# An expert FFN in float32: the first products of 64-row blocks as two halves of 32 rows in four column groups

## The chip, the cores and the metric

The kernel runs on one NeuronCore of a Trainium2 chip. Its engines are TensorE (PE in the profile; its weight loads are PEld), VectorE (DVE), ScalarE (ACT), GpSimd (POOL) and SyncE (SP), which issues most of the transfers. The metric is the device time of one execution in microseconds. Three runs of the kernel before took 1034.02, 1034.72 and 1036.19 us; the median is 1034.72 us.

## What is computed

The program takes 625 nodes of 768 features and 20,000 edges, and computes two residual layers in float32. The first is a graph attention network of two layers. The second is a transformer block: causal attention with 12 heads, then a mixture of 8 experts of which each row uses one. The change lies in the experts:

```python
gate_logits = h2 @ Wg
w, sel = jax.lax.top_k(gate_logits, 1)
hid = jax.nn.relu(jnp.einsum('nd,edf->enf', h2, W1) + b1[:, None, :])   # 768 -> 3072
y = jnp.einsum('enf,efd->end', hid, W2) + b2[:, None, :]                # 3072 -> 768
moe = jnp.einsum('ne,end->nd', combine, y)
```

The kernel computes for each row only the expert that it chose. The weights of an expert, W1 and W2, are 9.4 MB each.

## The kernel before

The early part of the program, up to the choice of the experts at about 630 us, is not touched. By then the rows have been written to memory sorted by expert. The first expert's first 128 rows are computed in straight code (`first_step`). All other rows go through a loop (L1498) whose number of passes and whose branches depend on the data: each pass handles one expert, with a block of 128 rows, one of 64, or none, and before it, as the table says, a block of 32. One word of the table says which (`w & 2`: 64 rows, `w & 4`: 128, `w & 1`: 32).

SBUF holds one set of an expert's weights, as six pieces: `w1[0..2]` and `w2[0..2]`, each for 1024 of the 3072 hidden features. As soon as PE no longer needs a half of a piece, SP issues the transfer of the next expert's half into the same place (`load_first` for W1, L1110, in halves of three of the six k; `load_second` for W2, L1120). These transfers are conditional: where the next pass uses the same expert they move nothing.

A 64-row block goes through class `Wide` with M = 64, P = 2 column groups. `into` (L1187) makes the first products: the stationary operand is 64 rows of `xT`, the moving one 512 columns of W1, and two such products lie side by side in the two column groups, with the result in PSUM as rows by hidden features (128 partitions are 2 x 64 rows). VectorE copies this to SBUF (`hb`, L1190). `turn` (L1198) transposes it on TensorE, four 128x128 tiles for each 1024 hidden features, since the second product needs the hidden features on the partitions; ScalarE then adds the bias and applies ReLU on the way from PSUM to `hT` (L1203). `out_of` (L1213) makes the second products with 64 columns of `hT` as the stationary operand, accumulating all three pieces in `pw`. The order on PE is written out by hand: `begin` is into(0), into(1), turn(0), into(2); then comes the block of 32, if there is one; `end` is out_of(0), turn(1), turn(2), out_of(1), out_of(2).

The block of 32 rows (`narrow`) already works in another way: with 32 rows as the stationary operand, four products of 256 columns lie in four column groups (L1461), and one VectorE instruction (L1463) turns the whole result in blocks of 32x32 out of PSUM, so that there is no copy and no turn on TensorE. ScalarE then adds the bias and applies ReLU in place (L1465). Its second products are at L1476.

The order of instructions is by hand for PE and SP; the other engines' order is made by the scheduler. Branches are taken by each engine's own sequencer: L1511 is the one before the 64-row `begin`, L1518 the one before the 32-row block, L1541 the one before the 64-row `end`.

Of the kernel before, what the change touches and what calls it, by code (L numbers as in the profile page):

```python
# [9 lines left out]
F32 = mybir.dt.float32  # L10
# [4 lines left out]
AF = mybir.ActivationFunctionType  # L15
# [10 lines left out]
KD = D // 128  # L26
# [15 lines left out]
B = 128  # L42
NS = E + N // B
SHUFFLE = (0, 3, 2, 4, 1, 5, 6, 7)
Q = 32
# [5 lines left out]
NFC = DF // FC  # L51
NK = DF // 128
BH = E * NK // 2
BLK = FC // 128
# [11 lines left out]
def gnn_moe_kernel(ctx: ExitStack, tc: tile.TileContext, p, out):  # L66
    nc = tc.nc
# [26 lines left out]
    def halves(name, w, k, n):  # L94

        r = k // 2 * 128
        return [wload(f"{name}{i}", k // 2, n,
                      w[i * r:(i + 1) * r, :].rearrange("(k p) n -> p k n", p=128))
                for i in range(2)]
# [51 lines left out]
    with tc.tile_pool(name="gnn", bufs=1) as gp:  # L151
# [31 lines left out]
        with tc.tile_pool(name="oneh", bufs=12) as op_, \  # L183
# [15 lines left out]
            w1 = halves("w1", p["L0_gnn_W1"], KD, HC)  # L199
# [253 lines left out]
            with tc.If(ok == 0):  # L453

                nc.vector.memset(C, 0.0)
                for a in range(0, EJ, PART):
                    clear()
                    for q in range(a, a + PART):
                        g, j = q // GJ, q % GJ
                        ohs = step(past[:, g, j:j + 1], True)  # L460
                        ohd = target(N, dst[:, g, j:j + 1], upper[:, g, j:j + 1])
                        for t in range(T):
                            nc.tensor.matmul(cps[:, t, :SH + 1], ohd[:, cols(t)], ohs, start=False,
                                             stop=False, skip_group_check=True)
# [14 lines left out]
        with tc.tile_pool(name="gw", bufs=2, reuse_waits="tile") as gw, \  # L479
# [13 lines left out]
            class Messages:  # L493


                def __init__(self, t, heads):
                    self.t, self.heads = t, heads
                    self.neg = gw.tile([R, N], F32, name="neg", bufs=1)
                    nc.vector.tensor_scalar(self.neg, C[:, t, :], 0.0, NEG, op0=OP.is_equal,
                                            op1=OP.mult)  # L500
                    self.tot = small.tile([R, HEADS], F32, name="tot")
                    self.z, self.zT, self.agg = {}, {}, None
# [45 lines left out]
            w2 = halves("w2", p["L0_gnn_W2"], KH, D)  # L548
# [93 lines left out]
            tp = ps.tile([128, 8, 128], F32, tag="p2", name="tpa")  # L642
# [54 lines left out]
    with tc.tile_pool(name="att", bufs=1, reuse_waits="tile") as a1, \  # L697
# [11 lines left out]
        def head_weights(name, w, which=(0, 1)):  # L709
            got = []  # L710
            for i in which:
                t_ = wp.tile([128, 3072], F32, tag="w", name=f"{name}{i}")
                v_ = t_[:, :KD * 384].rearrange("p (k n) -> p k n", k=KD)
                for k in range(KD):
                    nc.sync.dma_start(
                        v_[:, k, :].rearrange("p (h s) -> p h s", h=6),
                        w[6 * i:6 * i + 6, k * 128:(k + 1) * 128, :].rearrange("h p s -> p h s"))
                got.append(v_)
            return got
# [11 lines left out]
        hT = ap.tile([128, KD, N], F32, tag="xT", name="hT")  # L731
# [37 lines left out]
        v = a1.tile([R, T, D], F32, name="v")  # L769
        w = head_weights("L0_ffn_Wv", p["L0_ffn_Wv"])  # L770
        for t in range(T):
            for i in range(2):
                pp = ps.tile([128, 512], F32, tag="p1", name="pv")
                for c in range(KD):
                    nc.tensor.matmul(pp[:R, :384], hT[:, c, cols(t)], w[i][:, c, :],
                                     start=(c == 0), stop=(c == KD - 1))
# [326 lines left out]
    w1, w2 = [None] * NFC, [None] * NFC  # L1103
# [27 lines left out]
    sp = ctx.enter_context(tc.tile_pool(name="sps", bufs=2, space=PSUM, reuse_waits="tile"))  # L1131
# [10 lines left out]
    hT = [mw.tile([128, 4, 128], F32, name=f"hT{c}", bufs=1) for c in range(2 * NFC)]  # L1142
    pw = [sp.tile([128, 512], F32, name=f"pw{i}", bufs=1) for i in range(2)]
# [21 lines left out]
    class Wide:  # L1165
# [53 lines left out]
        def begin(self):  # L1219
            self.into(0)  # L1220
            self.into(1)
            for c in range(2, self.n):
                self.turn(c - 2)
                mm = self.into(c)
            return mm

        def end(self):
            n = self.n
            self.out_of(0)
            self.turn(n - 2)  # L1230
            self.turn(n - 1)
            for c in range(1, n):
                mm = self.out_of(c)
            return mm

    def prepare(rows, idx, M):

        nc.vector.tensor_copy(idx[:M], rows.bitcast(I32)[:M, D:D + 1])
        nc.vector.tensor_add(rows[:M, :D], rows[:M, :D], b2b[:M])
# [50 lines left out]
    bT, _ = biases(first_a)  # L1290
# [15 lines left out]
    for i, n in ((0, T), (1, TA)):  # L1306
        for s in range(n):
            nc.tensor.matmul(pc[:1, i * E:(i + 1) * E], ones[:, :1], oh[:, s, :], start=(s == 0),
                             stop=(s == n - 1))

    def row8(name, *shape, tag=None):
        return ap.tile([1, *shape], F32, name=name, tag=tag or name)
# [7 lines left out]
    v = nc.vector  # L1320
# [10 lines left out]
    key = row8("key", E)  # L1331
# [31 lines left out]
    for i in range(3):  # L1363
        s = 1 << i
        a = row8(f"inc{i}", E)
# [29 lines left out]
    begin, n_first, odd, its_number, from_row = (its[:, i, :] for i in range(5))  # L1395
# [16 lines left out]
    a = tabf[:, 0, :]  # L1412
    v.scalar_tensor_tensor(a[:, :NS], its_number, 2.0, tabf[:, 1, :NS], op0=OP.mult, op1=OP.add)
    w = tabf[:, 2, :NS]
# [11 lines left out]
    xT = free[:, U * Q * KD:2 * U * Q * KD].rearrange("p (k r) -> p k r", k=KD)  # L1426
# [26 lines left out]
    def narrow(bT, *then):  # L1453

        def into(c):
            ph = sp.tile([128, 4, 128], F32, tag="tp", name="phq").rearrange("p a b -> p (a b)")[:, :BLK * Q]
            w = w1[c].rearrange("p k (j g r) -> p k j g r", g=4, r=Q)
            v = ph.rearrange("p (j r) -> p j r", r=Q)
            for k in range(KD):
                for g in range(4):  # L1460
                    nc.tensor.matmul(v[g * Q:(g + 1) * Q], xT[:, k, :Q], w[:, k, :, g],  # L1461
                                     start=(k == 0), stop=(k == KD - 1))
            turned = nc.vector.transpose(hq[:, c * BLK:(c + 1) * BLK], v)  # L1463
            for j in range(c * BLK, (c + 1) * BLK):
                nc.scalar.activation(hq[:, j, :], hq[:, j, :], AF.Relu, bias=bT[:, j:j + 1])  # L1465
            return turned

        with tc.manual_schedule(engines={PE}):
            for c in range(NFC):
                turned = into(c)  # L1470
        load_first(*then)
        with tc.manual_schedule(engines={PE}):
            order = [(c, j, i) for c in range(NFC) for j in range(0, BLK, 4) for i in range(2)]
            for c, j, i in sorted(order, key=lambda o: o[0] and 1 + o[2]):
                for g in range(4):
                    nc.tensor.matmul(  # L1476
                        pq[i][g * Q:(g + 1) * Q, :384], hq[:, c * BLK + j + g, :],
                        w2[c][:, j + g, i * 384:(i + 1) * 384], start=(c == 0 and j == 0),
                        stop=(c == NFC - 1 and j == BLK - 4))
        with tc.issue_after(turned.ins):  # L1480
            prepare(rq, iq, Q)
        yq = rq[:, :D].rearrange("p (i c) -> p i c", i=2)
        for i in range(2):
            nc.vector.tensor_add(rs[:, i, :], yq[:, i, :], pq[i][:2 * Q, :384])  # L1484
            nc.vector.tensor_add(rs[:, i, :], rs[:, i, :], pq[i][2 * Q:, :384])  # L1485
            nc.vector.tensor_add(yq[:Q, i, :], rs[:Q, i, :], rs[Q:, i, :])  # L1486
# [11 lines left out]
    with tc.For_i(0, n_blk, 1, iteration_sync="reg_based") as i:  # L1498
        w = word(i)
        then = (w >> 4) & 7, (w >> 3) & 1  # L1500
        row, row_next = (nc.values_load(table[0:1, 1, ds(k, 1)], engines=[pool], min_val=0,
                                        max_val=NR - U * Q) for k in (i, i + 1))

        rows_in(row_next)
        nc.gpsimd.dma_start(rw, xr[ds(row + Q, B), :])
        nc.gpsimd.dma_start(rq[:Q], xr[ds(row, Q), :])
        bT, s = biases((w >> 8) & 7)
        tc.add_manual_dep(s.ins, first_load.ins.name, ORDER)
        of = {M: Wide(M, xT[:, :, Q:Q + M], bT) for M in (64, B)}

        with tc.If((w & 2) == 2) as c64:  # L1511
            with tc.manual_schedule(engines={PE}):
                of[64].begin()
        with c64.Else():
            with tc.If((w & 4) == 4):
                with tc.manual_schedule(engines={PE}):
                    of[B].begin()
        with tc.If((w & 1) == 1) as c32:  # L1518
            narrow(bT, *then)
        with c32.Else():  # L1520
            nc.vector.memset(iq, N)
            load_first(*then)
        turn_next()

        def scatter_narrow(*others):
            s = scatter_out(rq, iq, Q)
            for o in others:
                tc.declare_no_dep(s.ins, o.ins, reason="other rows")
            tc.add_manual_dep(s.ins, first_load.ins.name, ORDER)

        def finish(M):
            prepare(rw, iw, M)
            with tc.manual_schedule(engines={PE}):
                of[M].end()
            load_second(*then)
            add_up(rw, pw, M)
            s = scatter_out(rw, iw, M)
            tc.add_manual_dep(s.ins, first_made.ins.name, ORDER)
            scatter_narrow(s)

        with tc.If((w & 2) == 2) as d64:  # L1541
            finish(64)
        with d64.Else():
            with tc.If((w & 4) == 4) as d128:
                finish(B)
            with d128.Else():
                nc.gpsimd.dma_start(idle, xr[0:1, :8])
                load_second(*then)
                scatter_narrow()
# [31 lines left out]
```

## Time and profile before

The profiled execution took 1035.84 us; its span, from the first to the last instruction, is 1034.0 us, with a mean granted TensorE clock of 0.983.

| | busy us | share of the span | instructions |
|---|---|---|---|
| PE (matmul) | 971.3 | 94% | 4655 |
| PEld (weight loads) | 595.9 | 58% | 4656 |
| DVE | 460.1 | 44% | 1340 |
| ACT | 301.5 | 29% | 753 |
| POOL | 76.9 | 7% | 129 |

The DMA queues moved 195.07 MB in all, 174.78 of it on queue q1, which carries the weights. In the profile a line such as `688.12 10.52 PE L1187 MATMUL ph<-ew,xid 128*64 128x512 f32 x48 [0.99 <-SPq L1498]` is read as follows: start in us from the start of the span, duration of the merged group, engine, line of the kernel, operation, what is written and read, the shape of the stationary operand (128 deep by 64 columns) and of the moving one (128x512), how many instructions, and in brackets how long the engine was idle before and what ended that. In the groups of instructions the numbers after the bar are busy time in us, mean ns of one, and idle time before. In the windows the last three columns are granted TensorE clock, busy share of the 16 DMA engines, and GB/s. A float32 product appears as two matmul records and two weight loads.

### The profile page before, as it was taken

What the parts mean: (1) busy time and instruction counts of PE and PEld (TensorE: products, weight loads), DVE (VectorE), ACT (ScalarE), POOL (GpSimd) and SP (SyncE); (2) the same over time, 40 slices, a digit from 0 to 9 for tenths busy, and PEclk for the clock granted to TensorE, in tenths of its full rate; (3) what the DMA queues carried; (4) which work ended last, traced back from release to release, by engine and by line L of the source; (5) the groups of instructions that cost most, each with busy time, mean ns of one, the idle gap of its engine ahead of it and who ended that gap; (6) DMA issues with size and microseconds to landing.
All of it is one profiled execution on the core that took longest, in us unless ns stands there. A gap on an engine that the chain in (4) does not pass through costs nothing. (4 is left out here: it accounts for less than half of the span.)

```text
span 1034.0 us, 14964 instructions
## 1 busy us (share of the span) xinstructions
PE 971.3 (94%) x4655; PEld 595.9 (58%) x4656; DVE 460.1 (44%) x1340; ACT 301.5 (29%) x753; POOL 76.9 (7%) x129
## 2 busy tenths in 40 slices
PE   6888999999999999999999889999999999999992
PEld 4455466577555555677775655545454646644552
DVE  7877697275376660284555464112111213111212
ACT  6667554263140120344442211101110121102020
POOL 1200100000000010000000021010101010110010
PEclk9999999999999999999999889999999999999997
DMA  9300410300150081999400579410689999999991
GB/s 280 148 1 1 165 31 1 138 1 1 48 104 1 20 210 36 364 413 381 181 1 1 203 241 352 151 42 15 236 314 321 388 375 409 367 374 402 409 388 33
DMA packets 86880, 195.07 MB, mean 189 GB/s; under 512 B 32989, under 2 KB 34660, under 8 KB 86825
## 3 DMA queue, kind: packets, MB, share of 16 engines
q1 hardware_dynamic: 80073, 174.78, 47.2%
q0 software_dynamic: 6672, 19.44, 6.1%
q8 instruction: 29, 0.48, 0.2%
q14 instruction: 26, 0.21, 0.1%
q10 hardware_dynamic: 80, 0.16, 0.1%
HBM read 213.34 MB, written 39.55 MB: 245 GB/s over the span
## 5 line engine op out<-in xcount | busy, mean ns | idle before, releaser
L1213 PE MATMUL pw<-ew,hT 128*64 128x384 f32 (+1 forms) x672 | 160.2, 488 | 4.9 <-PEq L1518 2.0
L1213 PEld LDWEIGHTS pw<-ew,hT 128*64 128x64 f32 (+1 forms) x672 | 100.0, 160 | 59.5 <-issue 15.8
L1187 PE MATMUL ph<-ew,xid 128*64 128x512 f32 (+1 forms) x432 | 127.7, 594 | 1.8 <-SPq L1498 1.0
L1203 ACT ACTIVATE hT<-tph,bT 128x64 f32<-128x64 f32 (+1 forms) x168 | 41.0, 361 | 288.5 <-PE tph L1198 194.4
L1187 PEld LDWEIGHTS ph<-ew,xid 128*64 128x64 f32 (+1 forms) x432 | 53.6, 155 | 65.1 <-issue 58.1
L1190 DVE COPY hb<-ph 128x512 f32<-128x512 f32 x30 | 20.6, 691 | 137.0 <-PE ph L1187 137.0
L533 PE MATMUL agg<-xl,zT 125*125 125x256 f32 (+1 forms) x300 | 79.8, 417 | 1.3 <-ACT zT L522 1.1
L533 PEld LDWEIGHTS agg<-xl,zT 125*125 125x125 f32 x300 | 54.5, 188 | 19.6 <-ACT zT L522 2.6
L1250 DVE TENSOR_TENSOR rw<-rw,pw 64x192 f32<-64x192 f32 (+1 forms) x48 | 12.9, 315 | 106.0 <-PE pw L1213 105.7
L360 PE MATMUL pp<-w,yT 128*125 128x512 f32 x120 | 56.0, 606 | 0.0
L235 ACT ACTIVATE step<-iota,past 125x314 f16<-125x314 f16 x120 | 55.9, 548 | 0.0
L633 PE MATMUL ph<-wr,h1T 128*125 128x384 f32 x160 | 52.8, 486 | 0.0
L595 PE MATMUL ph<-w,h1T 128*125 128x384 f32 x160 | 52.4, 486 | 0.0
L252 PE MATMUL cps<-step,oh 125*125 125x314 f16 x181 | 37.1, 307 | 10.5 <-ACT step L235 7.4
L857 DVE CUSTOM_DVE_ANT_0 e<-sc,later 125x625 f32<-125x625 f32 (+4 forms) x60 | 29.8, 542 | 36.2 <-PE sc L841 36.2
L924 PE MATMUL po<-wpj,aT 128*125 128x384 f32 x120 | 42.8, 505 | 0.4 <-DVE xx L928 0.4
L861 ACT ACTIVATE e<-e,of 125x625 f32<-125x625 f32 (+4 forms) x60 | 35.7, 596 | 23.3 <-DVE of L857 23.2
L170 PE MATMUL ph<-wr,yT 128*125 128x512 f32 x96 | 42.1, 593 | 0.1
L595 PEld LDWEIGHTS ph<-w,h1T 128*125 128x125 f32 x160 | 30.0, 188 | 21.2 <-issue 0.5
L245 DVE TENSOR_SCALAR oh<-iota,drel,upper 125x125 f16<-125x125 f16 x160 | 41.1, 316 | 2.2 <-PE cps L252 2.1
L633 PEld LDWEIGHTS ph<-wr,h1T 128*125 128x125 f32 x160 | 29.8, 188 | 20.8
L252 PEld LDWEIGHTS <-oh 125*125 125x125 f16 x181 | 24.9, 140 | 26.6 <-DVE oh L245 13.6
(344 smaller groups left out, 1336.4 us busy)
## 6 DMA issues: line engine op xcount, KB each, us to landing
ew<-in_L_ffn_W_dram SPq DMA_DIRECT2D x108, 1536.0 KB
xr<-zt SPq DMA_DIRECT2D x5, 3076.0 KB
xg<-zt SPq DMA_DIRECT2D x5, 3072.0 KB
w<-in_L_gnn_W_dram SPq DMA_DIRECT2D x4, 1536.0 KB
wr<-in_L_gnn_Wr_dram SPq DMA_DIRECT2D x4, 1536.0 KB
xid<-xg POOLq DMA_DIRECT2D x32, 120.0 KB, 6.5
b2b<-in_L_ffn_b_dram SPq DMA_DIRECT2D x9, 384.0 KB
rw<-xr POOLq DMA_DIRECT2D x7, 384.5 KB, 7.8
```

What stands on the lines that cost most here:

```text
L170: nc.tensor.matmul(pp[:R, :], yT[:, c, cols(t)], part(wr1, KD, c, i, 512), start=(c == 0), stop=(c == KD - 1))
L235: nc.scalar.activation(o, iota[:, :SH + 1], AF.Sign, bias=at, scale=-1.0)
L245: m = nc.vector.tensor_scalar(o, iota[:, :n], at, weight, op0=OP.is_equal, op1=OP.mult)
L252: nc.tensor.matmul(where, target(R, d[:, j:j + 1], w[:, j:j + 1]), step(s[:, j:j + 1], j % 4 != 3), start=False, stop=False, skip_group_ch ...
L360: nc.tensor.matmul(pp[:R, :], yT[:, c, cols(t)], part(w1, KD, c, i, 512), start=(c == 0), stop=(c == KD - 1))
L533: nc.tensor.matmul(self.agg[:R, c0:c0 + n], zT[:, s, :], xl[:, s, x0:x0 + n], start=(s == 0), stop=(s == T - 1))
L595: nc.tensor.matmul(ph[:R, :384], h1T[:, c, cols(t)], part(w2, KH, c, i, 384), start=(c == 0), stop=(c == KH - 1))
L633: nc.tensor.matmul(ph[:R, :384], h1T[:, k, cols(t)], part(wr2, KH, k, i, 384), start=(k == 0), stop=(k == KH - 1))
L924: nc.tensor.matmul(po[t, i][:R, :384], aT[:, c, cols(t)], wpj[i][:, c, :], start=(c == 0), stop=(c == KD - 1))
L1187: mm = nc.tensor.matmul(ph[g * M:(g + 1) * M, :C].rearrange("p (j f) -> p j f", f=128), self.xT[:, k, :], w[:, k, g], start=(k == 0), stop ...
L1203: self.made = nc.scalar.activation(hT[c][:, k, r], tp[:, k, r], AF.Relu, bias=self.bT[:, f:f + 1])
L1213: mm = nc.tensor.matmul(pw[i][g * M:(g + 1) * M, :384], hT[c][:, k, g * M:(g + 1) * M], w[:, self.block(c, g, k), i * 384:(i + 1) * 384], ...
```

## The change

Class `Halves` takes the place of `Wide` for blocks of 64 rows. For each piece of 1024 hidden features it makes the first products twice, once for rows 0 to 31 and once for rows 32 to 63, in four column groups (`into32`, which is also what the block of 32 now calls). VectorE turns each half's result out of PSUM into `hT`, 64 columns for each 128 hidden features; ScalarE adds the bias and applies ReLU in place in SBUF. `begin` now makes all three pieces, and `end` only the second products; their shapes, 64 columns by 384, stay, with other pairs of 128 features side by side. The copies to `hb` and the turns on TensorE are gone for these blocks. Blocks of 128 rows and the straight code are as before.

```diff
+    def into32(c, ph, cols, xT):
+        w = w1[c].rearrange("p k (j g r) -> p k j g r", g=4, r=Q)
+        v = ph[:, :BLK * Q].rearrange("p (j r) -> p j r", r=Q)
+        for k in range(KD):
+            for g in range(4):
+                nc.tensor.matmul(v[g * Q:(g + 1) * Q], xT[:, k, cols], w[:, k, :, g],
+                                 start=(k == 0), stop=(k == KD - 1))
+        return v
+
+    class Halves:
+
+        def __init__(self, xT, bT):
+            self.xT, self.bT = xT, bT
+
+        def begin(self):
+            for c in range(NFC):
+                h = hT[c].rearrange("p a b -> p (a b)").rearrange("p (j r) -> p j r", j=BLK)
+                for r in (slice(0, Q), slice(Q, 2 * Q)):
+                    nc.vector.transpose(h[:, :, r], into32(c, sp.tile([128, 512], F32, name="ph"), r,
+                                                           self.xT))
+                for j in range(BLK):
+                    f = c * BLK + j
+                    nc.scalar.activation(h[:, j, :], h[:, j, :], AF.Relu, bias=self.bT[:, f:f + 1])
+
+        def end(self):
+            M = 2 * Q
+            for c in range(NFC):
+                h = hT[c].rearrange("p a b -> p (a b)").rearrange("p (j r) -> p j r", j=BLK)
+                order = [(j, i) for j in (0, 4, 1, 5) for i in range(2)]
+                for j, i in sorted(order, key=lambda o: o[1]) if c == NFC - 1 else order:
+                    for g in range(2):
+                        nc.tensor.matmul(
+                            pw[i][g * M:(g + 1) * M, :384], h[:, j + 2 * g, :],
+                            w2[c][:, j + 2 * g, i * 384:(i + 1) * 384], start=(c == 0 and j == 0),
+                            stop=(c == NFC - 1 and j == 5))
...
-        of = {M: Wide(M, xT[:, :, Q:Q + M], bT) for M in (64, B)}
+        of = {64: Halves(xT[:, :, Q:Q + 64], bT), B: Wide(B, xT[:, :, Q:Q + B], bT)}
```

More of the change, by code (lines that the diff above doesn't have):

```diff
@@ L1455, in into @@
         def into(c):
[L1456 to L1462, printed above, removed]
+            ph = sp.tile([128, 4, 128], F32, tag="tp", name="phq").rearrange("p a b -> p (a b)")
+            v = into32(c, ph, slice(0, Q), xT)
             turned = nc.vector.transpose(hq[:, c * BLK:(c + 1) * BLK], v)
```

## The prediction, made before the changed kernel ran

> **What bounds the kernel now.** I read the page's slices first (PE at 9 to the end, DMA at 9 from about 775 us), then the order of PE's work in the expert loop, then the busy time by stretch, then the branches. The loop makes seven passes: 64 rows (from 688 us), 128 (723), 64 (789), 64+32 (823), 64 (876), 128+32 (911), 32 (997). So four passes use the changed code. PE in order of time, with the first pass, one block of 32 and the end:
>
> ```profile
> 688.12 10.52 PE L1187 MATMUL ph<-ew,xid 128*64 128x512 f32 x48 [0.99 <-SPq L1498]
> 698.57 0.66 PE L1198 MATMUL tph<-ident,hb 128*128 128x128 f32 x4
> 699.15 5.37 PE L1187 MATMUL ph<-ew,xid 128*64 128x512 f32 x24
> 705.21 2.12 PE L1213 MATMUL pw<-ew,hT 128*64 128x384 f32 x11 [0.68 <-PEq L1518]
> 707.56 3.76 PE L1213 MATMUL pw<-ew,hT 128*64 128x384 f32 x21 [0.23 <-issue]
> 711.25 1.09 PE L1198 MATMUL tph<-ident,hb 128*128 128x128 f32 x8
> 712.50 10.69 PE L1213 MATMUL pw<-ew,hT 128*64 128x384 f32 x64 [0.16 <-issue]
> 723.12 10.57 PE L1187 MATMUL ph<-ew,xid 128*128 128x512 f32 x24
> ...
> 839.67 7.98 PE L1461 MATMUL phq<-ew,xid 128*32 128x256 f32 x144
> 847.46 4.68 PE L1476 MATMUL pq<-ew,hq 128*32 128x384 f32 x50
> 854.52 4.27 PE L1476 MATMUL pq<-ew,hq 128*32 128x384 f32 x46 [2.38 <-DMA ew<-in_L_ffn_W_dram]
> ...
> 1012.65 5.97 PE L1476 MATMUL pq<-ew,hq 128*32 128x384 f32 x46 [3.29 <-DMA ew<-in_L_ffn_W_dram]
> ```
>
> Until 851 us PE never waits for weights; from there on it does, in passes 4 to 7 (2.38; 0.95; 0.82 and 2.10; 3.29 us). The second-to-last column of the windows, DMA share, says from where the transfers set the pace:
>
> ```profile
> 760.00:770.00 10.00, 10.00 (x38) 6.15 (x36) 0.17 (x1) 2.18 (x8) 0.00 (x0) 1.00 0.89 316
> 780.00:790.00 10.00, 10.00 (x33) 5.47 (x33) 1.49 (x8) 0.00 (x0) 0.00 (x0) 1.00 0.90 308
> 790.00:800.00 10.00, 10.00 (x50) 3.44 (x46) 1.16 (x3) 0.00 (x0) 4.52 (x7) 1.00 0.98 337
> 800.00:900.00 100.00, 95.83 (x670) 59.50 (x669) 24.68 (x48) 18.37 (x85) 11.63 (x17) 1.00 1.03 382
> 900.00:1010.00 110.00, 104.65 (x689) 58.37 (x685) 18.17 (x41) 20.05 (x85) 10.44 (x16) 1.00 1.03 391
> ```
>
> Before 790 the engines stand idle a tenth of the time, since each half piece of weights waits for PE to finish with the old one. From about 795 to 1010 they never do, and the last half piece, issued at 996.21, lands at 1012.5, so some 12 us of other transfers were queued before it. Hence only what moves PE before 795 (passes 1 and 2, and the release of weights early in pass 3) moves the end; of the four changed passes only the first counts in full.
>
> **What PE saves.** The shapes, from the groups of instructions:
>
> ```profile
> L1187 PE MATMUL ph<-ew,xid 128*64 128x512 f32 x288 | 63.8, 594 | 1.0 <-SPq L1498 1.0
> L1461 PE MATMUL phq<-ew,xid 128*32 128x256 f32 x432 | 23.9, 380 | 0.8 <-DVE rw L1250 0.8
> L1463 DVE STREAM_TRANSPOSE hq<-phq 128x256 f32<-128x256 f32 x9 | 4.0, 450 | 18.8 <-PE phq L1461 18.8
> ```
>
> A product in f32 is two passes, each with its weight load. Per 64-block and piece the old form has 24 passes: 63.8 / 12 = 5.32 us busy. The new form is what the 32-blocks already do, twice: 23.9 / 9 = 2.66 us a half, 5.31 us a piece. The streaming is equal; the four column groups really run together. What goes is the turning. First products: 688.12 to 704.52 = 16.40 us before; twice the 32-block's 7.98 = 15.96 after: -0.44. Second products: the gap for two turns, 711.25 to 712.50, is -1.25. In the first pass alone the second products also stumble: the first piece takes 6.04 us (705.21 to 711.25) against 5.41 in pass 3 (806.20 to 811.61), as code is being fetched there; that 0.63 should go, since the code in question is by then fetched. Saved in pass 1: 0.44 + 1.25 + 0.63 = 2.32 us; in passes 3, 4 and 5 1.69 each, under the transfers.
>
> The rest is covered. VectorE turns each half in 450 ns against a half's 2.66 us of products, with two PSUM tiles. ScalarE's eight activations of a piece run at 1.75 us (pass 1, 699.43) in either form, and the last piece's are needed only after two pieces of second products, 10.5 us later; without that cover they would cost 2 us a block. The queues of SP and POOL issue the same transfers in the same order.
>
> The Trainium skill speaks against this form ("TensorEngine Tiling (Array Packing)", PSUM Bottleneck): after a fourfold packing the emptying of PSUM may become the limit. Row L1463 disagrees here, 0.45 of 2.66 us; by the rule the saving of 0.44 would go, no more.
>
> **What the longer code costs.** The built loop body holds 1734 PE instructions instead of 1331: a 64-block's first part is 144 products x 4 = 576 instructions in place of 36 x 4 and 4 turns x 2. Code comes in packets of 16384 bytes:
>
> ```profile
> q8 instruction: 29, 0.48, 0.2%
> L1518 PEldq COMPARE_BRANCH  x10: 78/178/3824, 700.5 to 1015.5; - x10
> ```
>
> Between such packets the trace has about 256 PE instructions (251, 259, 256 between 281.8 and 394.8 us). The last four start at 699.8, 701.5, 705.0 and 710.0: the first pass fetches the loop, and the later six find it there. The branch at L1518, which jumps over the 32-part, takes 0.18 us in the median and 3.82 in the first pass, where it waits for its target. It is hidden there: PE's sequencer left the first products at 700.09, 4.43 us before PE ended them (704.52), and the gap to the second products, 0.68, is no longer than in pass 3 (0.67). With the new form the sequencer is less far ahead. The nearest row is the 32-block: its closing branch stands at 856.19, PE's end at 858.79, 2.60 us or 32 passes of 81 ns. At 55 ns a pass (23.9 / 432) the lead is 1.8 us. From leaving to the resumed branch took 700.09 to 704.30 = 4.21; another 0.91 to the first product (705.21). So the gap is 4.21 - 1.8 + 0.91 = 3.3 us instead of 0.68: +2.6. The low end of a miss is the fetch at 705.0, which began with the resumed branch at 704.30 and let PE go on at 707.56, 3.26 us: 0.39 + 3.26 - 1.8 + 0.91 = 2.76, +2.1. The high end is two packets in turn, as the next block's goes first; with 0.8 of a second packet's duration of about 1 us added that is +3.4. I take +2.6, the row of the same branch.
>
> A long gap has a second price: after the 3.29 us wait at 1012.65 the granted clock was 0.5 for 3.4 us, and 46 passes took 5.97 us instead of 4.27: +1.70. After gaps of 2.38 and 2.10 us it stayed at 1.00. A gap of 3.3 must nearly fill one of the clock's 3.4 us steps for that, so one execution in three perhaps; I take 0 and keep 1.7.
>
> **What starts later.** Weights are released by halves of three k. The old form finishes with the first half after half a piece (2.6 us), the new one only in its second run through the piece (three quarters, 3.9): 1.3 us later. Where transfers are queued this is free. It bites once, in pass 3, where the first W1 half is issued at 792.79 and the engines have just run out (share 0.98 for 790 to 800). Between 0 and +1.3; I take +0.6, since a half's transfer is still running until about 795.5.
>
> **Sum.** -2.32 + 2.6 + 0.6 = +0.9 us. The profiled execution took 1035.84 us, 1.8 of it around its span of 1034.0; it would take 1036.7. The median of the runs is 1034.72, so 1.1 under that execution: forecast 1035.6.
>
> **Rivals.**
> - *The fetch stays hidden* (the sequencer keeps its 4.4 us lead, or the target is fetched early). For it: 20 passes of lead in the old form; against it, 32 short passes are but 1.8 us. -2.32 with 0 to +1.3: 1032.4 to 1033.7.
> - *The clock halves after the gap*: +0.9 + 1.7 = +2.6, 1037.3, to +4.7 at the upper ends (with the stumble kept).
> - *The loop no longer fits into PE's code memory.* It is slower then, and this is the rival on the far side. By the packet at 699.8, just before the 162nd instruction, the old loop lies across six blocks of 256 and the new one across eight. Six are held for sure (no packet after 710); for eight no row speaks. It decides if fewer than eight are held: then each jump over a part misses again. Pass 1 stays at +0.3; pass 2 jumps over the 64-part with a lead of 2.0 us (721.16 to 723.12), 4.21 - 2.0 = +2.2; pass 3 +2.6 on its way, partly under the transfers, and later ones wait for packets among full queues: +3 to +8, 1038 to 1043. The skill's "Runtime: NRT & Kernel Launch", Instruction fetch mechanics, gives PE 2048 instructions in such blocks, which the eight would just fill, so by it nothing is added; the same section also says only two blocks, which six passes without a packet contradict.
> - *All four passes count*, if the transfers follow PE after all: -2.32 - 3 x 1.69 = -7.4, 1027.3. Against it: share 1.03 for 210 us.
>
> **How the numbers follow.** Bound for "no change": 0.2%, 2.07 us, about what runs of this kernel (1034.02 to 1036.19) can tell. Forecast case 45% (-0.2 to +3.0: 39 same, 6 slower); halved clock 17% (4 same, 13 slower); hidden fetch 16% (4 faster, 12 same); code refetched 14% (slower); all passes 8% (faster). Together 12 faster, 55 same, 33 slower. The range runs from the hidden fetch, 1032.4, to 1039.8, which takes in the clock's upper end (1039.4) and some of the refetching; 8% lie below and about as many above.
>
> **What would show it.** In the profile after: 64-blocks' first products in 16 us without turns; second products in 15.8; a PE gap of about 3.3 us between them in the first pass and 0.7 later; more and later instruction packets, but none after the first or second pass; longer waits for weights in passes 4 to 7; an unchanged 1.03 share. Packets of q8 in every pass would make me wrong upwards; a gap under 1 us in the first pass, downwards.

## The result and the profile after

The changed kernel takes 1040.37 us (median; 1039.68 to 1041.20) against 1034.02 us (1032.44 to 1036.19) of the kernel before: a ratio of 1.006, 95% interval 1.0044 to 1.0075. It is slower, and 0.6 us above the upper end of the predicted range. The profiled execution took 1041.2 us, its span is 1039.0 (before: 1034.0). The medians lie 6.35 us apart and the two profiled spans 5.0; what follows accounts for the 5.0, and the rest is within the scatter of the runs (1032.44 to 1036.19 before).

PE in order of time, after (start, duration, engine, line, operation, tiles, shapes, count, idle time before):

```profile
688.57 15.75 PE L1242 MATMUL ph<-ew,xid 128*32 128x256 f32 x288 [0.99 <-SPq L1530]
708.88 18.69 PE L1268 MATMUL pw<-ew,hT 128*64 128x384 f32 x96 [4.57 <-PEq L1550]
727.50 10.57 PE L1187 MATMUL ph<-ew,xid 128*128 128x512 f32 x24
...
793.43 15.75 PE L1242 MATMUL ph<-ew,xid 128*32 128x256 f32 x288
810.03 15.80 PE L1268 MATMUL pw<-ew,hT 128*64 128x384 f32 x96 [0.85 <-DVE hT L1255]
825.76 15.75 PE L1242 MATMUL ph<-ew,xid 128*32 128x256 f32 x288
843.49 9.66 PE L1242 MATMUL phq<-ew,xid 128*32 128x256 f32 x144 [1.98 <-issue]
...
860.03 4.28 PE L1508 MATMUL pq<-ew,hq 128*32 128x384 f32 x46 [2.41 <-DMA ew<-in_L_ffn_W_dram]
...
904.80 2.80 PE L1268 MATMUL pw<-ew,hT 128*64 128x384 f32 x16 [0.28 <-DMA ew<-in_L_ffn_W_dram]
908.72 1.61 PE L1268 MATMUL pw<-ew,hT 128*64 128x384 f32 x8 [1.11 <-DMA ew<-in_L_ffn_W_dram]
912.63 5.79 PE L1268 MATMUL pw<-ew,hT 128*64 128x384 f32 x24 [2.31 <-DMA ew<-in_L_ffn_W_dram]
...
1017.60 5.97 PE L1508 MATMUL pq<-ew,hq 128*32 128x384 f32 x46 [3.14 <-DMA ew<-in_L_ffn_W_dram]
```

The reader is to compare the first two rows with the pair at 793 and 810. It is the same work; in pass 1 the gap between first and second products is 4.57 us instead of 0.85, and the second products take 18.69 us instead of 15.80. The windows of after say why they are longer (third column from the right: granted clock):

```profile
704.00:709.00 5.00, 0.43 (x10) 0.15 (x3) 1.25 (x3) 2.02 (x8) 0.92 (x1) 0.90 0.04 7
709.00:712.00 3.00, 3.00 (x10) 1.76 (x12) 2.03 (x3) 0.00 (x0) 0.00 (x0) 0.50 0.00 0
712.00:716.00 4.00, 4.00 (x18) 2.41 (x16) 0.00 (x0) 0.00 (x0) 0.00 (x0) 0.64 0.00 0
716.00:720.00 4.00, 4.00 (x28) 2.60 (x26) 0.00 (x0) 0.00 (x0) 0.00 (x0) 1.00 0.02 4
```

The clock is 0.5 from 708.0 for 6.8 us. And the gap is the branch before the 32-block, which waits for the code behind it once (minimum, median and maximum in ns), as in the kernel before, where its longest was 3824:

```profile
L1550 PEldq COMPARE_BRANCH  x10: 78/177/4688, 703.3 to 1019.9; - x10
```

The page's row for code packets shows two more than before (29), and in the trace none falls between 717.9 and 1040.7: after pass 1 nothing is fetched again.

```profile
q8 instruction: 31, 0.51, 0.2%
```

Where the span's 5.0 us come from, by starts and ends of these rows:

| | before | after | change |
|---|---|---|---|
| start of the loop | 688.12 | 688.57 | +0.45 |
| pass 1 | 35.00 | 38.93 | +3.93 |
| pass 2 | 66.00 | 65.93 | -0.07 |
| start of pass 3 to the last landing | 223.53 | 224.17 | +0.64 |
| from there to the end | 21.35 | 21.40 | +0.05 |

Four fifths lie in pass 1, where the new form saves: first products 16.40 to 15.74 (-0.66); gap 0.68 to 4.57 (+3.89); second products 17.91 to 18.62 (starts to next start), of which, against the 15.80 of pass 3, -2.11 for turns and stumble and +2.82 for the clock. -0.66 + 3.89 - 2.11 + 2.82 = +3.94.

One thing was not expected: SP issues the first W1 transfer of pass 3 at 804.87, 11.4 us into the pass, instead of 3.7. SP's transfers, before:

```profile
792.79 14.62 SPq L1110 DMA_DIRECT2D ew<-in_L_ffn_W_dram  x6
```

and after:

```profile
804.87 8.13 SPq L1110 DMA_DIRECT2D ew<-in_L_ffn_W_dram  x6
```

The DMA share (second-to-last column) is lower meanwhile, 0.83 for 1.03 between 795 and 810. Pass 3 starts 4.3 us later after the change, so a fairer pair is the first 19 us of the pass, where the share is 0.86 for 1.00. Windows of before:

```profile
795.00:810.00 15.00, 14.33 (x74) 6.65 (x72) 4.60 (x7) 1.75 (x8) 3.56 (x6) 1.00 1.03 347
810.00:1010.00 200.00, 191.15 (x1309) 112.94 (x1305) 38.86 (x83) 36.67 (x160) 21.15 (x32) 1.00 1.03 389
```

and of after:

```profile
795.00:810.00 15.00, 14.18 (x264) 8.29 (x257) 2.88 (x7) 4.15 (x17) 4.53 (x7) 1.00 0.83 287
810.00:1010.00 200.00, 189.05 (x1684) 111.28 (x1688) 42.55 (x92) 35.37 (x144) 20.50 (x31) 0.98 1.03 394
```

### The profile page after: what moved, and what is told of

Its sections match the earlier page's. It is cut to its first block, busy times and chain, and to the rows that moved or that the text cites. A ratio compares the mean times of both kernels' runs of the same rounds, so it can differ in the third digit from the quotient of the medians.

```text
span 1039.0 us, 16644 instructions
## 1 busy us (share of the span) xinstructions
PE 970.3 (93%) x5471; PEld 601.9 (58%) x5472; DVE 462.6 (45%) x1352; ACT 305.3 (29%) x753; POOL 77.6 (7%) x129
## 5 line engine op out<-in xcount | busy, mean ns | idle before, releaser
L1213 PE MATMUL pw<-ew,hT 128*128 128x384 f32 x288 | 95.0, 487 | 1.0 <-DVE hb L1190 1.0
L1268 PE MATMUL pw<-ew,hT 128*64 128x384 f32 x384 | 68.5, 514 | 10.0 <-PEq L1550 4.6
L1213 PEld LDWEIGHTS pw<-ew,hT 128*128 128x128 f32 x288 | 53.9, 190 | 37.7 <-issue 2.4
L1203 ACT ACTIVATE hT<-tph,bT 128x128 f32<-128x128 f32 x72 | 20.4, 374 | 169.6 <-PE tph L1198 169.6
L1242 PE MATMUL ph<-ew,xid 128*32 128x256 f32 x1152 | 63.0, 379 | 1.0 <-SPq L1530 1.0
L1187 PE MATMUL ph<-ew,xid 128*128 128x512 f32 x144 | 63.7, 594 | 0.0
L1268 PEld LDWEIGHTS pw<-ew,hT 128*64 128x64 f32 x384 | 42.3, 144 | 35.5 <-issue 26.5
L1259 ACT ACTIVATE hT<-hT,bT 128x64 f32<-128x64 f32 x96 | 24.2, 334 | 121.7 <-DVE hT L1255 121.7
L1242 PEld LDWEIGHTS ph<-ew,xid 128*32 128x32 f32 x1152 | 39.0, 110 | 25.4 <-issue 1.7
L857 DVE CUSTOM_DVE_ANT_0 e<-sc,later 125x625 f32<-125x625 f32 (+4 forms) x60 | 29.8, 543 | 36.2 <-PE sc L841 36.2
L1187 PEld LDWEIGHTS ph<-ew,xid 128*128 128x128 f32 x144 | 26.6, 190 | 30.8 <-issue 30.8
```

Of the source, the lines that this page charges most:

```text
L1187: mm = nc.tensor.matmul(ph[g * M:(g + 1) * M, :C].rearrange("p (j f) -> p j f", f=128), self.xT[:, k, :], w[:, k, g], start=(k == 0), stop ...
L1213: mm = nc.tensor.matmul(pw[i][g * M:(g + 1) * M, :384], hT[c][:, k, g * M:(g + 1) * M], w[:, self.block(c, g, k), i * 384:(i + 1) * 384], ...
L1242: nc.tensor.matmul(v[g * Q:(g + 1) * Q], xT[:, k, cols], w[:, k, :, g], start=(k == 0), stop=(k == KD - 1))
L1268: nc.tensor.matmul(pw[i][g * M:(g + 1) * M, :384], h[:, j + 2 * g, :], w2[c][:, j + 2 * g, i * 384:(i + 1) * 384], start=(c == 0 and j == ...
```

## The experiments

Theory: the loss is the one late fetch of code behind the branch, which shows because PE's sequencer, which runs ahead by a number of passes, is ahead by less time when the passes are short; and the clock that falls behind the gap. Rivals: the column groups or the longer code as such; the later release of W1; refetching. All ratios are to the kernel before, run on the same chip, with 95% intervals. "Pass 1" is the time from the first product of the loop to the first of pass 2.

| kernel | pass 1, us | gap before the second products | clock behind it | ratio |
|---|---|---|---|---|
| before | 35.0 | 0.68 | 1.00 | 1 |
| changed | 38.9 | 4.57 | 0.5 for 6.8 us | 1.006 (1.0044 to 1.0075) |
| wide_last | 35.4 | 0.84, then 1.70 | 1.00 | 1.0009 (0.999 to 1.0028) |
| wide_first | 40.9 | 6.34 | 0.5 for 6.8 us | 1.0079 (1.0048 to 1.011) |
| short_lead | 43.7 | 4.64 | 0.5 for 6.8 us | 1.0125 (1.0094 to 1.0157) |
| fill_gap | 37.6 | 0.75 | 1.00 | 1.0036 (1.0016 to 1.0057) |
| fill_half | 36.7 | 2.47 | 1.00 | 1.0043 (1.0021 to 1.0065) |
| early_out | 36.0 | 2.71 | 0.5 for 3.4 us | 1.006 (1.0045 to 1.0076) |
| hint | 35.6 | 2.77 | 0.5 for 3.4 us | 1.0061 (1.0046 to 1.0075) |
| split_narrow | 33.4 | 0.97 | 1.00 | 1.011 (1.0077 to 1.0143) |
| early_release | 38.9 | 4.52 | 0.5 for 6.8 us | 1.006 (1.004 to 1.0081) |

### Where the short passes stand: wide_last and wide_first

The two put one of the three pieces back into the old form: the last one, or the first one.

```diff
         def begin(self):
-            for c in range(NFC):
...
+            self.piece(0)
+            self.piece(1)
+            self.wide.into(2)
```

> The first two pieces of a 64-row block as halves of 32 rows, the third in the old form (64 rows, copy, turn on TensorE). Theory (short lead): with the last products in the old form PE's sequencer is again about 4.4 us ahead when it leaves them, so the first pass's fetch of the code behind the jump hides; PE gap between first and second products of pass 1 about 0.7 us, clock 1.00 there, pass 1 about 33.5 us (35.0 before, 38.9 with all halves), time about 1033.3 us, 0.7 under the kernel before. Rival 1 (products in four column groups are themselves slower or lower the clock): two thirds of the 6 us loss stay, about 1038. Rival 2 (weights released later starve the transfers): the first piece is released as late as with all halves, so about 1040.

```diff
         def begin(self):
-            for c in range(NFC):
...
+            self.wide.into(0)
+            self.piece(1)
+            self.wide.turn(0)
+            self.piece(2)
```

> The same work and nearly the same number of PE instructions (1596 in the loop against 1595) as with the third piece in the old form, but here the first piece is in the old form and the other two are halves. Theory (short lead): the last products are short passes, so the sequencer is only about 1.4 us ahead, the gap in pass 1 is about 4.6 us, the clock falls to 0.5 after it, pass 1 takes about 39 us and the time is about 1039.5 us. Rival 1 (column groups themselves): as with the third piece in the old form, about 1038 in both. Rival 2 (late release): the first piece is released early again, so about 1034.

PE in pass 1 of wide_last:

```profile
698.92 5.37 PE L1187 MATMUL ph<-ew,xid 128*64 128x512 f32 x24
705.13 0.51 PE L1275 MATMUL pw<-ew,hT 128*64 128x384 f32 x1 [0.84 <-DVE hb L1190]
707.33 5.48 PE L1275 MATMUL pw<-ew,hT 128*64 128x384 f32 x31 [1.70 <-issue]
```

and of wide_first:

```profile
701.71 5.39 PE L1242 MATMUL ph<-ew,xid 128*32 128x256 f32 x96
713.43 7.72 PE L1213 MATMUL pw<-ew,hT 128*64 128x384 f32 x32 [6.34 <-PEq L1563]
```

Both kernels hold the short passes in two pieces of three and about the same amount of code (1595 and 1596 PE instructions in the loop). With 512-wide passes last, the branch is taken at 700.24, 4 us before PE is done, and its 3.77 us are hidden; with short passes last they are not. So it is the passes just ahead of the branch that decide, and not the column groups or the length. Both cost more than expected: in wide_last the code of the second products comes one packet late (the 1.70, where the kernel before loses 0.23 at that place); in wide_first the branch is through at 709.5, but a further packet is fetched at 710.3 before PE goes on at 713.43, and the gap is 6.34. wide_last is level with the kernel before.

### The kernel before with short passes: short_lead

```diff
             with tc.manual_schedule(engines={PE}):
                 of[64].begin()
+                for _ in range(24):
+                    nc.tensor.matmul(pw[0][:64, :8], ident[:, :64], hb[0][:, :8], start=True, stop=True)
```

> The kernel before with 24 tiny products (128x64 by 128x8, 48 short passes) put behind the first products of each 64-block; they are made and thrown away, and nothing else is changed: no column groups, no halves, copies and turns as before. Theory (the sequencer's lead, in passes, decides whether the fetch of the branch's target shows): the short passes cost 1.3 to 2.6 us in pass 1, and the lead before the branch falls from 4.43 to under 2.5 us, so the gap behind them grows from 0.68 to 3 to 4.6 us and the granted clock falls to 0.5 after it: the second products 2 to 3 us longer. Pass 1 takes 40 to 44 us instead of 35.0, the kernel 1039 to 1043. Rival (the long gap comes from the column groups or from the longer code of the new form): gap under 1 us, clock 1.00, pass 1 36.3 to 37.6, the kernel 1036 to 1037.5.

```profile
704.56 2.94 PE L1515 MATMUL pw<-hb,ident 128*64 128x8 f32 x48 [0.91 <-DVE hb L1190]
712.13 7.02 PE L1213 MATMUL pw<-ew,hT 128*64 128x384 f32 x32 [4.64 <-PEq L1520]
...
817.78 7.07 PE L1213 MATMUL pw<-ew,hT 128*64 128x384 f32 x32 [0.64 <-PEq L1520]
```

This is PE in passes 1 and 3. Nothing of the change is in this kernel, and the gap is there, 4.64 us, in the first pass only. That shows the cause without the column groups. The total missed its forecast (1047.3 against 1039 to 1043): with the 24 products passes 3 to 5 are also 5.4, 3.6 and 4.2 us longer than before, and from pass 3 on PE no longer waits for weights anywhere, so the cover was used up. Also, 2.94 us of 8-column passes with 0.91 and 0.64 us of gap around them were followed by a halved clock in pass 3 (0.5 from 817.7 for 3.4 us), so its clock in pass 1 is not the gap's doing alone.

### Filling the gap: fill_gap, fill_half and early_out

Products of 128x64 by 128x512 are put behind the first products and thrown away: six, or three.

```diff
         def begin(self):
             for c in range(NFC):
...
+            for _ in range(6):
+                nc.tensor.matmul(pw[0][:64], ident[:, :64], hb[0], start=True, stop=True)
```

> All halves, and after a 64-block's first products six more products of 128x64 by 512 whose result is thrown away: 12 passes of 0.43 us, 5.2 us more PE work in each of the four passes with 64 rows. Theory (short lead, then the halved clock): the added passes cover the fetch in pass 1, PE gap 0.7 us, clock 1.00, second products 16 us instead of 18.6; pass 1 about 37.5 us instead of 38.9, and what is added in passes 3 to 5 lies under the transfers: about 1039 us, although 21 us of work are added. Rival 1 (column groups lower the clock): second products stay at 18.6 us, about 1042. Rival 3 (all passes count): 1056 to 1061.

> The changed kernel with 3 products of 128x64 by 128x512, made and thrown away, behind the first products of each 64-block: half the filling of fill_gap (about 2.7 us instead of 5.36). Theory: the branch still takes 4.7 us, the gap is 4.57 - 2.7 = 1.9 us, which is under the 2.4 us behind which the clock has stayed at 1.00, so the second products take 15.8 and not 18.6: pass 1 15.75 + 2.7 + 1.9 + 15.8 = 36.2 us, 2.7 less than the changed kernel, 1.4 less than fill_gap; the kernel 1037 to 1038. Rival (the clock follows the idle share over a longer time, or the fetch itself, and not the length of the gap): clock 0.5 for some 3 us or more, second products 17 or more, pass 1 over 37.5, the kernel 1039 or more.

PE in pass 1 of fill_gap:

```profile
704.33 5.36 PE L1267 MATMUL pw<-hb,ident 128*64 128x512 f32 x12
710.45 15.87 PE L1275 MATMUL pw<-ew,hT 128*64 128x384 f32 x96 [0.75 <-PEq L1561]
```

and of fill_half:

```profile
703.47 2.79 PE L1267 MATMUL pw<-hb,ident 128*64 128x512 f32 x6
708.73 15.80 PE L1275 MATMUL pw<-ew,hT 128*64 128x384 f32 x96 [2.47 <-PEq L1561]
```

Both passes come out as forecast (37.6 for 37.5; 36.7 for 36.2). Doing 5.36 us of useless work shortens pass 1 by 1.3 us, as the clock stays at 1.00 and the branch (4.68 and 5.02 us) lies under it. The gap of 2.47 left the clock alone here, by a little luck: the clock goes in steps of 3.41 us (last section), and the edge of one at 708.25 cut the gap into 1.99 and 0.48 us. The median of fill_half, 1039.11, is 1 us above its forecast and by itself fits the rival's "1039 or more"; its interval (0.2% each way) takes in both. Pass 1 and the clock decide against the rival.

In early_out the filling is work that is needed anyway, the first third of the second products:

```diff
         def begin(self):
             for c in range(NFC):
...
+            self.out_of(0)
...
         def end(self):
-            for c in range(NFC):
+            for c in range(1, NFC):
```

> The changed kernel with the first third of the second products of each 64-block (32 passes, 5.25 us) moved ahead of the branch that jumps over the 32-block: the filling of fill_gap, but with work that is needed anyway. Theory: the fetch of 4.7 us lies under it, gap under 1.2 us, clock 1.00; pass 1 takes 15.75 + 5.3 + 0.8 + 10.5 = 32.3 us, 6.6 less than the changed kernel and 2.7 less than the kernel before; the kernel 1032 to 1035. Rival (what counts is when W1 is released: the first transfer of pass 3 now waits for the 117th product of 160, some 13 us into the pass, and the block of 32 in pass 4 starts 5.3 us later): pass 1 as above, but the stretch from the start of pass 3 to the last landing grows from 224.2 to 227 us or more, the kernel 1036 or more.

```profile
703.89 5.38 PE L1268 MATMUL pw<-ew,hT 128*64 128x384 f32 x32
711.98 12.34 PE L1268 MATMUL pw<-ew,hT 128*64 128x384 f32 x64 [2.71 <-PEq L1554]
```

The same 5.4 us of filling, and still a gap of 2.71, so the forecast failed (pass 1 36.0 us for 32.3, the kernel 1039.54 for 1032 to 1035). In fill_gap it is 12 passes, in early_out 32: the sequencer left at 703.54 there, 6.15 us before PE's end, and at 705.89 here, 3.38 us. From leaving to the resumed branch took 5.17 and 5.14 us. So what covers a fetch is not how long the work ahead of the branch takes, but how long its last 20 or so passes take (19 to 27, last section). Pass 3 to the last landing grew to 226.1 us (790.18 to 1016.29), so the rival has a part in the total too; early release and the 32-block's later start are not told apart there.

### The code: hint, split_narrow and even_counts

hint asks for the branch's target early:

```diff
         with tc.If((w & 2) == 2) as c64:
+            tc.mark_branch_hint_location("past_narrow", engines=[PE])
...
-        with tc.If((w & 1) == 1) as c32:
+        with tc.If((w & 1) == 1, label="past_narrow") as c32:
```

> The changed kernel with one instruction more on PE: at the start of a 64-block's first products a hint names the branch that jumps over the 32-block, so that its target can be fetched 14 us before it is needed; products, their order and the loads stay. Theory (all that the change loses in pass 1 is this one late fetch and the clock behind it): gap between first and second products 0.8 to 1.2 us instead of 4.57, granted clock 1.00, second products 15.8, pass 1 32 to 33 us instead of 38.9 (before: 35.0); with 0.6 to 1 us for the late release of W1 the kernel takes 1032.5 to 1034.5, level with the kernel before or a little faster. Rival (the code of the second half is late whatever is asked for, since the fetches come one after another, or a hint for a branch other than the next one does nothing): gap 3 us or more, the kernel 1039 to 1041.

```profile
707.25 17.18 PE L1268 MATMUL pw<-ew,hT 128*64 128x384 f32 x96 [2.77 <-ACTq L1551]
...
886.82 17.79 PE L1242 MATMUL ph<-ew,xid 128*32 128x256 f32 x288 [5.91 <-issue]
```

The gap shrank to 2.77, but the fetch did not come early: a packet at 704.1, when the branch was reached. What went is its companion. In the changed kernel two packets start at 703.92 and 704.28 and take 1.57 and 1.84 us; here one starts at 704.08 and takes 0.96, and the branch 2.91 us instead of 4.69. Also, code was fetched again later, 47 packets in all, above all at the loop's closing branch of pass 4:

```profile
L1530 PEldq COMPARE_BRANCH  x8: 91/230/7348, 683.0 to 1022.2; - x8
```

Why the companion went and why code was fetched again isn't shown. The theory failed; the time, 1040.41 us, is the rival's, but its gap of 3 us or more did not come, and pass 1 (35.6 us) got shorter while later passes lost it again.

split_narrow makes the jump short instead: the 32-block's first products go ahead of the large block's, its second products and first loads stay behind, and the 128-row branch goes ahead of the 64-row one.

```diff
+        with tc.If((w & 1) == 1):
+            narrow(bT)
-        with tc.If((w & 2) == 2) as c64:
+        with tc.If((w & 4) == 4) as c128:
...
         with tc.If((w & 1) == 1) as c32:
-            narrow(bT, *then)
+            narrow_end(*then)
```

> The changed kernel with the 32-block's first products moved ahead of the large block's, and its second products and the first loads behind them, and with the 128-row branch ahead of the 64-row one: behind the 64-row first products PE now jumps over some 220 instructions instead of the whole 32-block, so the target of the jump lies in the packet that comes next anyway. All 64-blocks are in halves. Theory (only the miss of the branch's target and the clock behind it cost anything): gap under 1.2 us, clock 1.00, second products 15.8; pass 1 31.5 to 33.5 us instead of 38.9; the kernel 1032 to 1034.5, since the later first loads may give some of it back. Rival (a miss comes wherever PE first jumps ahead by more than the packet in hand): the miss moves to the new jumps ahead of the first products, where the sequencer has no lead left after the start of the loop, or stays at 3 us or more: pass 1 36 us or more, the kernel 1036 or more.

PE in pass 1 and in pass 6:

```profile
705.18 15.80 PE L1268 MATMUL pw<-ew,hT 128*64 128x384 f32 x96 [0.97 <-DVE hT L1255]
721.89 10.54 PE L1187 MATMUL ph<-ew,xid 128*128 128x512 f32 x24 [0.91 <-DVE rw L1287]
...
926.63 2.58 PE L1242 MATMUL phq<-ew,xid 128*32 128x256 f32 x24 [3.56 <-DMA ew<-in_L_ffn_W_dram]
932.34 2.79 PE L1242 MATMUL phq<-ew,xid 128*32 128x256 f32 x24 [3.12 <-DMA ew<-in_L_ffn_W_dram]
```

Pass 1 is what the change promised once the miss is gone: 33.4 us against 35.0, clock 1.00. But the kernel is the slowest but two, because of its order: in pass 6 the 32-block's first products now use up the three W1 pieces in the time that they take to land, with waits of 2.17, 2.02, 3.56, 3.12 and 1.07 us, 11.9 in all, where the 128-block used to spread them over 32 us. The expectation had overlooked that.

even_counts puts 92 tiny products behind the first products of the 128-block. It was made for the release (below), and showed the refetch rival by accident.

```diff
             with tc.If((w & 4) == 4):
                 with tc.manual_schedule(engines={PE}):
                     of[B].begin()
+                    for _ in range(92):
+                        nc.tensor.matmul(pw[0][:64, :8], ident[:, :64], hb[0][:, :8], start=True, stop=True)
```

> The changed kernel with 92 tiny products (128x64 by 128x8), made and thrown away, behind the first products of each 128-block, so that both branches hold 144 products on PE. Theory (after the two branches SP waits for one count for both, and the branch with fewer products is padded to the count of the other, ahead of its own; so the wait for the 9th product of a 128-block's 52 has become one for the 101st of a 64-block's 144): with equal counts the first W1 transfer in pass 3 is issued within 5 us of the start of the pass instead of 11.4. The tiny products cost 5 to 8 us in pass 2, so the kernel's time says nothing; from the start of pass 3 to the last landing takes 223 to 224 us instead of 224.2 if the late issue cost anything there. Rival (the release waits for the products of both halves, whatever the counts): the issue stays at 8 us or more into the pass.

```profile
q8 instruction: 81, 1.33, 0.5%
...
L1268 PE MATMUL pw<-ew,hT 128*64 128x384 f32 x384 | 68.5, 519 | 42.3 <-issue 31.5
```

These are rows of its page. The loop has 368 PE instructions more, 2102 in place of 1734, and the kernel takes 1158.34 us, a ratio of 1.1196 (1.114 to 1.1252): 81 packets in place of 31, and fetches in every pass. PE stands idle for 42.3 us ahead of the 64-blocks' second products (10.0 in the changed kernel), mostly with nothing to wait for but code. The median of the loop's closing branch goes from 0.23 to 1.61 us. The tiny products were slower than expected (16.56 and 16.51 us in the two passes with 128 rows, for 5 to 8, at half clock from the fourth us on), but of the 123 us over the kernel before that explains 33. The rest are the waits for code and the half clock that follows them (mean clock 0.927 for 0.983), not told apart. So 1734 instructions were held and 2102 were not; the count alone doesn't decide, since hint, with one instruction more than 1734, fetched code again too. The Trainium skill's "Runtime: NRT & Kernel Launch", Instruction fetch mechanics, gives PE 2048, and the two runs stand on either side of that.

### The release of W1: early_release and even_counts

early_release interleaves the two halves over k, so that the first half of a piece is finished after half the piece, as in the old form.

```diff
-                for r in (slice(0, Q), slice(Q, 2 * Q)):
-                    nc.vector.transpose(h[:, :, r], into32(c, sp.tile([128, 512], F32, name="ph"), r,
-                                                           self.xT))
...
+            for half, ks in ((a, range(3)), (1 - a, range(3)), (1 - a, range(3, KD)), (a, range(3, KD))):
```

> All halves, but the two halves of a piece take turns: k 0 to 2 of one, k 0 to 2 of the other, then k 3 to 5 of that and of the first, so that half of a piece's weights is released after half of its products, as in the old form. Theory: only the start of the saturated transfers in pass 3 moves, by 0.6 us: about 1039.8 us, pass 1 still with a gap of 4.6 us. Rival 2 (late release starves the transfers): 1034 to 1036.

It changed nothing: PE as in the changed kernel, and SP's first W1 transfer still at 804.80:

```profile
708.79 18.71 PE L1282 MATMUL pw<-ew,hT 128*64 128x384 f32 x96 [4.52 <-PEq L1568]
```

In the changed kernel's trace every PE product counts one counter up. The 64-row branch now has 144 products ahead of the merge (40 before), the 128-row branch 52. By the theory the one with fewer is padded to the same count, the padding first, and SP's wait, which stands behind the merge, holds one number for both, the larger: 92 + 9 = the 101st product of 144, whose count is at 804.86. The padding itself can't be seen in the trace, but the same sum names the product whose count comes last before the issue in other runs too: the 65th of 108 in wide_last, the 107th of 150 in fill_gap, the 117th of 160 in early_out. SP's transfers in even_counts, where both branches have 144:

```profile
831.20 0.37 SPq L1120 DMA_DIRECT2D ew<-in_L_ffn_W_dram  x1
835.23 13.66 SPq L1110 DMA_DIRECT2D ew<-in_L_ffn_W_dram  x6
```

Pass 3 starts at 831.00 there; the first W1 transfer follows 4.2 us in instead of 11.4, and the others at PE's pace. That shows the counts as the cause. What the late issue costs can't be read from this run, as its passes wait for code.

## Why the prediction was wrong

- *What bounds it.* Right in the main: PE's work in passes 3 to 5 shrank and the end did not follow. Only pass 3 became shorter as a whole, though (34.08 to 32.33 us); pass 4 went from 52.43 to 54.11 and pass 5 from 35.65 to 38.48. The waits for weights in passes 4 to 7 grew from 9.5 to 10.4 us in sum: most in pass 5 (0.28 + 1.11 + 2.31 for 0.95), while pass 6 waited less (1.15 for 0.82 + 2.10). The DMA share did not stay unchanged: it fell early in pass 3.
- *What PE saves.* Right for pass 1: first products 15.75 for a forecast 15.96, turns gone, stumble gone, second products 15.80; 0.66 + 2.11 = 2.77 against 2.32. VectorE's turn at 0.45 us did not bind. What ScalarE does was not all covered, as was held: its eight activations took 2.02 us and not 1.75, and in pass 4, where the block of 32 comes next, PE's sequencer stood until 843.33, just after the fourth of the last eight ended (843.28). That is the gap of 1.98 us at 843.49, and the half clock behind it added 1.68. PE waited 2.41 us for weights after that, so it cost the end nothing. Why these products wait for ScalarE is open.
- *What the longer code costs.* Two terms failed, and this is the first: +2.6, with +3.4 as its highest, and +3.89 measured. The mechanism was right and the size off. The lead was 1.48 us for a forecast 1.8 (702.83 to 704.31), and from leaving to the resumed branch took 5.19 us for 4.21. Here two packets travel together, and the branch took 4.69 us with the pair and 2.91 with one, in hint; that the two slow each other is read from these times and not tested alone. The forecast had priced the second packet only as the upper end, and at 0.8 of its own length.
- *The clock, taken as 0 and named as a rival at 17%.* This is the second term that failed, and with +2.82 the larger. The 0 rested on the step that a gap must nearly fill one of the clock's steps of 3.4 us, so that 3.3 us would bring it once in three. The traces show that some 2.0 us of idle time within one step are enough (last section). As an estimate from this, a gap of 3.3 us escapes only where an edge cuts it into two parts that are both under 2.0, in 0.7 of 3.41 positions or one in five; a gap of 4.57 never does. So the half clock was the likely case even at the forecast's own gap. The price was higher too, 6.8 us at half speed, +2.82, instead of 3.4 and +1.70: the gap ran 0.86 us into the next step. It was there with every gap over 4.5 of the table, and the mean clock of all five runs of the changed kernel, 0.974 to 0.977 for 0.983 before, agrees.
- *What starts later.* The stretch grew by 0.64 for a forecast +0.6, but that is luck, since the reason was wrong. Weights are not released by halves of a piece but by a count that is shared with another branch; the issue came 7.8 us later and not 1.3. Its price is not settled. In the profiled executions the stretch from pass 3 to the last landing is 223.5 us with the issue 3.7 us into the pass (before), 221.9 at 7.6 (wide_last), 224.2 at 11.4 (changed), 224.5 at 11.4 (early_release), 223.7 at 11.6 (fill_half), 225.4 at 12.0 (fill_gap), 225.3 at 12.3 (wide_first) and 226.1 at 13.2 (early_out): some of the share lost before 810 is made up for later (394 GB/s for 389), and one execution of each does not say more.
- *The rivals.* The fetch stayed exposed. All passes counting fell. Refetching did not come at 1734 instructions; where it came, at 2102, some 90 us came with it (123 less the 33 of the added products). The rival's 3 to 8 us were priced for this kernel's own code, so that price was not put to the test.

The sum with the measured sizes is -2.77 + 3.89 + 2.82 + 0.64 = +4.6 of the span's +5.0; 0.45 of the rest was there when the loop began.

## What to carry over

A branch whose target was not yet fetched cost 2.9 to 5.0 us once in these kernels, and the sequencer's lead hides it; that lead was 19 to 27 passes whatever they lasted, so replacing long matrix products by short ones of equal streaming time can expose it. Put long passes just ahead of a far jump, and price a miss with the pair of packets and with the halved clock behind the gap. Where a loop's branches merge, look at what the counted waits behind them wait for before adding products to one branch.

## What the runs showed of the hardware

- The lead, from the sequencer's leaving to PE's end of the work, in passes: 20 in the kernel before (4.43 us of 223 ns), 20 in early_out (3.38 us of 168), 27 in the changed kernel (1.48 us of 55), 19 in short_lead (1.17 us of 61).
- The granted clock changed only on a grid of 3.41 us: in the changed kernel it fell at 708.02, 844.55 and 912.82, 40 and 20 steps apart, and so on in every trace after 660 us. What decided was PE's idle time within one such step, and not the length of a gap. Leave out the steps with 8-column products. Of the others that began at clock 1.00, each with 2.07 us or more of idle time was followed by half clock and none with 1.97 or less; of those between, two with 1.98 were (pass 4 of the changed kernel and of early_release) and two with 1.99 and 2.01 were not (fill_half, pass 1; even_counts). The half clock lasted a second step where the first still held 0.82 us or more, and ended where it held 0.74 or less. So gaps of 1.98 and 2.31 us in passes 4 and 5 of the changed kernel brought it (843.49 above, 9.66 us for 7.98 of work; 912.63, 5.79 for 4.09), and gaps of 2.47 and 2.41 elsewhere did not. The Trainium skill ("TensorE: Matmul & The Clock Gate", HAM oscillation) warns of idle gaps over some 3.4 us; the runs here show the price from 2 us on.
- Products of 8 columns, back to back, did not keep the clock up: in even_counts it fell 3.9 us after their start at 774.04, with no idle time between.
- With the branch hint the fetch did not start early; the companion packet did not come, and code that the changed kernel held was fetched again in later passes.
